# One-core decoder layer: the first two batches normalised in halves with their copies and first projections in another order, and the last product's last two batches in PSUM tiles of their own

## The chip, the cores and the metric

The kernel runs on one core of a Trainium2 chip; the other seven cores are idle. The metric is the device time of one execution in microseconds (us). The core has five engines, each with a queue of instructions that it works off in order: TensorE (PE, matrix products; the loading of weights is listed as PEld), VectorE (DVE), ScalarE (ACT), GpSimd (POOL), and SyncE (SP), which here only issues transfers (DMAs). They wait for one another through semaphores. PE writes its results to PSUM; DVE and ACT carry them from there to SBUF.

## The reference

A decoder layer in float32 over x of shape 16 x 128 x 1024 (16 batches of 128 tokens, 1024 features):

```python
x = x + attn(layernorm(x))          # one head of width 256, softmax over 128 keys
x = x + xattn(layernorm(x), ctx, ctx)   # 8 heads, linear attention over the channels
x = x + ffn(layernorm(x))           # int4 weights, dequantised; silu(gate) * up, then down

# the parts that the change touches
def layernorm(x, eps=1e-5):
    return (x - mean(x)) / sqrt(var(x) + eps)
def attn(x):                        # qkv: 1024 -> 3 * 256
    q, k, v = split(x @ Wqkv + bqkv)
    return softmax(q @ k.T / sqrt(256)) @ v @ Wo + bo
def ffn(x):                         # inter = 2752
    return (silu(x @ Wg.T) * (x @ Wu.T)) @ Wd.T
```

## The kernel before

**The stages.** Self-attention comes first; cross-attention and the dequantising of the weights follow; the feed-forward network takes most of the time. Its products are built by a fast scheme with seven smaller products in place of eight, at two levels, so a part of a result is a sum of several products that stay in PSUM or in SBUF tiles until the last one is there.

**The start (lines 361 to 431 and 523 to 543).** SP's queue loads the first four batches of x, then the weights `wqkv` in five pieces, `bv`, the next four batches, `wo`, the bias `bo_sb` (128 copies of one row, line 379), and the last eight batches. Self-attention works in four groups of four batches (512 tokens), the loop `for t in range(NT)`. For a group, each batch is normalised to `xn` (128 tokens x 1024), turned by eight 128 x 128 transposes on PE into two PSUM tiles `tr` (four transposes each), and copied into the group's `xnT`: the first half by DVE, the second half by ACT. The pool of `tr` tiles has three, and the pool of `xn` has two, so the sixth `tr` needs the copy of the third to be over, and so on.

The first group has a function of its own, `first_rows` (line 396). DVE takes the statistics of a half batch at a time (`half`: BATCH_NORM_STATS2), then the aggregate, and DVE and POOL form the reciprocal deviation `rstd` (POOL raises to the power -0.5, line 153); ACT normalises the batch in one instruction of 1024 columns (`rows`), PE turns it, ACT copies the second half and DVE, one batch later, the first half (`copy`). The wrapper `InOrder` keeps the DVE instructions in the order in which they are written; instructions without it are ordered by the framework's scheduler.

Then the projection of queries and keys: four output parts f, each over eight chunks of features. For the first group each part is made in two halves, first the 256 tokens of batches 0 and 1, then those of batches 2 and 3 (`query_key` with `tokens`). One chunk of 256 tokens is two matmul instructions in the trace, so half a part is 16. Between the second halves of the parts stand, for f = 0 to 3: `add_bias(f)` on POOL (line 434: X[b] = X[b] + bo_sb, 128 x 1024, in place) and `turn` of batch 4 + f, whose normalising is done by DVE (line 156, `xn<-X,mv,rstd`). Before the projection stand the statistics of batches 4 to 7 and one `row_rstd` for all four (lines 152 and 153, a row of 128 x 4).

**The end (lines 1922 to 1998).** The down projection ends with the seven inner products `INNER = (1, 5, 6, 7, 3, 4, 2)` of the last outer product. A PSUM tile `po` holds four batches x 256 columns. Product 2 is accumulated on the tile of product 1. In the last product the first two batches are multiplied, and `got` adds them to the sum `u` and sends them out; then the other two in the same tile, the same way. Batches 0 and 2 leave through ACT's queue, 1 and 3 through SP's.

Of the kernel before, what the change touches and what calls it, by code (L numbers as in the profile page):

```python
# [12 lines left out]
F32 = mybir.dt.float32  # L13
# [6 lines left out]
P = 128  # L20
# [63 lines left out]
def decoder_layer(  # L84
# [59 lines left out]
    def row_stats(b, vector=nc.vector):  # L144
        st = small.tile([P, 2, 6], F32, name="bnst")
        for h in range(2):
            vector.bn_stats(st[:, h, :], X[b][:, ts(h, 512)])
        vector.bn_aggr(mv[:, b, :], st)

    def row_rstd(b0, n, vector=nc.vector, gpsimd=nc.gpsimd):  # L150
        r = rstd[:, ds(b0, n)]
        vector.tensor_scalar(r, mv[:, ds(b0, n), 1], EPS, None, ALU.add)
        gpsimd.tensor_tensor(r, r, mhalf[:, :n], ALU.pow)
# [14 lines left out]
    def normalise_act(dst, src, b, scalar=nc.scalar):  # L168
        scalar.activation(
            dst, src, AF.Identity, bias=shift[:, b : b + 1], scale=rstd[:, b : b + 1]  # L170
        )
# [183 lines left out]
    with (  # L355
# [27 lines left out]
        def turn_half(xn, xnT, b, h):  # L383
            tr = atr.tile([P, 4, P], F32, name="tr")
            for j in range(4):
                nc.tensor.transpose(tr[:, j, :], xn[:, ts(4 * h + j, P)], ident)  # L386
            return xnT[:, ts(h, 4), ts(b % BPT, S)], tr
# [8 lines left out]
        def first_rows(xnT):  # L396

            vector = InOrder(tc, nc.vector)
            halves = {}

            parts = {}

            def half(b, h):
                if h == 0:
                    parts[b] = small.tile([P, 2, 6], F32, name="bnst")
                vector.bn_stats(parts[b][:, h, :], X[b][:, ts(h, 512)])
                if h == 1:
                    vector.bn_aggr(mv[:, b, :], parts[b])
                    row_rstd(b, 1, vector)

            def rows(b):
                xn = a2.tile([P, C], F32, name="xn")
                row_shift(b, vector)
                normalise_act(xn, X[b], b)
                halves[b] = turn_half(xn, xnT, b, 0)
                nc.scalar.copy(*turn_half(xn, xnT, b, 1))

            def copy(b):
                vector.tensor_copy(*halves[b])

            half(0, 0)
            half(0, 1)
            for b in range(1, BPT):
                half(b, 0)
                rows(b - 1)
                if b > 1:
                    copy(b - 2)
                half(b, 1)
            rows(BPT - 1)
            copy(BPT - 2)  # L430
            copy(BPT - 1)

        def add_bias(b):
            nc.gpsimd.tensor_tensor(X[b], X[b], bo_sb, ALU.add)
# [86 lines left out]


        xnTs = [a2.tile([P, CC, TB], F32, name="xnT")]
        first_rows(xnTs[0])
        oT = None
        for t in range(NT):
            xnT = xnTs.pop()
            more = t + 1 < NT
            if more:
                xnTs.append(a2.tile([P, CC, TB], F32, name="xnT"))  # L530
                for b in range((t + 1) * BPT, (t + 2) * BPT):
                    row_stats(b)
                row_rstd((t + 1) * BPT, BPT)
            qkT = a2.tile([P, 4, TB], F32, name="qkT")
            halves = {}
            if t == 0:

                for f in range(4):
                    halves[f] = aps.tile([P, TB], F32, name="mm")
                    query_key(f, xnT, qkT, halves[f], ts(0, TB // 2))  # L540
            for f in range(4):
                if t == 0:
                    query_key(f, xnT, qkT, halves[f], ts(1, TB // 2))
                else:
                    query_key(f, xnT, qkT)
                add_bias(t * BPT + f)
                if more:
                    if oT is not None:
                        give((t - 1) * BPT + f, oT)
                    turn((t + 1) * BPT + f, xnTs[0])  # L550
                if t > 0:
                    for _ in range(2 if t == 2 else 1 + f % 2):
                        next(early, None)
            v = a2.tile([P, BPT, DH], F32, name="v")
            value(0, xnT, v)
            at = weigh(qkT)
            if more:
                value(1, xnT, v)
                value(2, xnT, v)
                atT = turn_weights(at)  # L560
                value(3, xnT, v)
                if t == 0:
                    for _ in range(3):
                        next(early)
            else:
# [1222 lines left out]
    with ExitStack() as dst:  # L1788
# [125 lines left out]
        for n, oq in enumerate(DOWN):  # L1914
            (lr, wr), (_, _, L, W) = rem, now
            direct(*now)
            after = None
            if n + 1 < len(DOWN):
                rem = remainder(DOWN[n + 1])
                keep_sums()  # L1920
                load_left(DOWN[n + 1], rem)
                after = operands(DOWN[n + 1])
                load_left(DOWN[n + 1], rem, True)
            bank, kept = {}, {}

            def multiply(bank, pairs, start, stop, rows=range(BPT)):
                for i in rows:
                    for c, (l, w) in enumerate(pairs):
                        nc.tensor.matmul(  # L1929
                            bank[:, i, :],  # L1930
                            l[:, ts(i, S)],
                            w,

                            start=(start and c == 0 and i % 2 == 0),
                            stop=(stop and c == len(pairs) - 1),
                            skip_group_check=True,
                        )

            for iq in INNER:
                set_ = {2: 1, 3: 5, 4: 7}.get(iq, iq)  # L1940
                if set_ == iq:
                    bank[iq] = dps[iq].tile(wide, F32, name=f"po{iq}")
                pairs = [(L[iq, i], W[iq, i]) for i in range(NI)]

                more = {2: (0, 0), 3: (0, 1), 4: (1, 0)}.get(iq)
                if more is not None:
                    pairs.append((lr[more[0]], wr[:, ts(more[1], OW)]))
                ps = bank[set_]
                if oq == DOWN[-1] and iq == INNER[-1]:
                    put_outs()  # L1950
                    for rows in (range(2), range(2, BPT)):
                        multiply(ps, pairs, False, True, rows)
                        got(oq, (0, 0), ps, only=rows)
                    break
                multiply(ps, pairs, set_ == iq, iq == 6 or more is not None)
                put_outs()
                if iq == 1:
                    t = kept["u"] = dt.tile(wide, F32, name="iu")
                    nc.scalar.copy(t, ps)
                elif iq == 5:  # L1960
                    combine(3, *now)
                    for ib in ((1, 1), (0, 1), (1, 0), (0, 0)) if oq == 4 else ():
                        vector.tensor_tensor(U[ib], U[ib], residual(oq, ib), ALU.add)
                elif iq == 6:
                    t = kept["u"]
                    vector.tensor_tensor(t, ps, t, ALU.add)
                    kept["v"] = dt.tile(wide, F32, name="iv", bufs=1)
                    vector.tensor_tensor(kept["v"], bank[5], t, ALU.add)
                elif iq == 7:
                    extra = dps[6].tile(wide, F32, name="po6")  # L1970
                    multiply(extra, [(lr[1], wr[:, OW:])], True, True)
                    got(oq, (1, 1), ps, kept["v"], extra)
                elif iq == 3:
                    got(oq, (0, 1), ps, kept["u"])
                elif iq == 4:
                    got(oq, (1, 0), ps, kept["u"])
                else:
                    got(oq, (0, 0), ps)
                if after is not None and iq in (3, 4, 2):
                    combine({3: 5, 4: 6, 2: 7}[iq], *after)  # L1980
            now = after
# [74 lines left out]
```

## Time and profile before

Three runs took 2171.88 us in the median (2171.53 to 2173.71). The profiled execution took 2173.11 us, with a span of 2171.3 us from its first to its last record.

| engine | busy us | share of the span |
|---|---|---|
| PE matmul | 2153.8 | 99% |
| PE weight loads | 1643.8 | 76% |
| DVE | 1556.3 | 72% |
| POOL | 803.9 | 37% |
| ACT | 525.5 | 24% |

| stretch, us | PE busy us of | DVE busy us | POOL busy us | DMA engines busy |
|---|---|---|---|---|
| 0 to 8.2 | 0.00 of 8.20 | 3.73 | 1.48 | 78% |
| 8.2 to 18.1 | 9.38 of 9.90 | 5.51 | 1.44 | 96% |
| 18.1 to 33.5 | 15.40 of 15.40 | 12.15 | 6.22 | all |
| 33.5 to 47.5 | 14.00 of 14.00 | 11.23 | 14.00 | 42% |
| 47.5 to 63.6 | 16.10 of 16.10 | 7.89 | 6.42 | 1% |
| 2159 to 2166 | 5.45 of 7.00 | 1.03 | 0.00 | 13% |

A row of the timeline is: start and duration in us, engine, line of the code, operation, what it writes from what it reads, shape, count, and in brackets how long the engine had been idle and what ended that. When a row has a count over 1, the duration is that of the whole group. A row of the chain has its start, its length, and the engine, tile and line. Matmuls overlap their neighbours, so the ends of PE rows are modelled.

### The profile page before, as it was taken

To read this page: it belongs to the slowest core of one execution; us is meant where nothing else is said; L and a number is where in the kernel's file an instruction comes from. 1 tells how busy PE (TensorE), PEld (TensorE's weight loads), DVE (VectorE), ACT (ScalarE), POOL (GpSimd) and SP (SyncE) were. 2 spreads that over 40 slices of the span, in tenths; PEclk is the share of its full clock that TensorE was granted. 3 is DMA by queue.
4 is the path that set the end of the run, shared out by engine and by line. 5 is a ranking of instruction groups with operands and counts; after the bars stand their busy time and mean duration, and the time that the engine had idled before them with its cause. 6 is when DMAs were issued, how large, how long until landed. Compare 5 with 4: busy or idle time off the path is not lost.

```text
span 2171.3 us, 25688 instructions
## 1 busy us (share of the span) xinstructions
PE 2153.8 (99%) x9004; PEld 1643.8 (76%) x9004; DVE 1556.3 (72%) x2098; ACT 525.5 (24%) x710; POOL 803.9 (37%) x675
## 2 busy tenths in 40 slices
PE   8999999999999999999999999999999999999998
PEld 7565655555555568888888888888886888888887
DVE  7899578888888758786777987878774445534573
ACT  2111235655665541211221212112111000000000
POOL 5454124333433345544444545444441022323200
PEclk9999999999999999999999999999999999999999
DMA  6446447777797676878888746677667578979941
GB/s 259 150 131 219 154 136 237 236 226 236 223 276 242 191 237 217 288 254 262 264 282 290 228 150 209 209 238 237 201 206 237 182 206 242 282 197 254 265 128 60
DMA packets 272203, 474.56 MB, mean 219 GB/s; under 512 B 29633, under 2 KB 128321, under 8 KB 266177
## 3 DMA queue, kind: packets, MB, share of 16 engines
q1 hardware_dynamic: 226736, 383.02, 54.6%
q0 software_dynamic: 27456, 71.45, 12.1%
q10 hardware_dynamic: 17872, 18.36, 2.6%
q8 instruction: 74, 1.21, 0.2%
q14 instruction: 65, 0.52, 0.1%
HBM read 314.64 MB, written 157.55 MB: 217 GB/s over the span
## 4 chain that ended last, share of the span: by engine, by line
PE 95%; DVE 3%; issue 1%; ACT 0%; POOL 0%; DMA 0%; DVEq 0%; POOLq 0%; ACTq 0%
PE q L80 38%; PE po L1929 22%; PE kq L80 10%; PE mm L80 8%; PE kx L80 5%; PE mm L441 4%; PE p L80 3%; PE mm L456 2%; PE mm L335 1%; DVE pa L80 1%; PE tr L386 0%; DVE C L80 0%; DVE pc L80 0%; PE mm L471 0%; PE mm L511 0%
## 5 line engine op out<-in xcount | busy, mean ns | idle before, releaser
L80 PE MATMUL q<-ti,li 128*128 128x256 f32 x1680 | 385.4, 379 | 0.0
L80 PEld LDWEIGHTS q<-ti,li 128*128 128x128 f32 x1680 | 319.2, 190 | 43.4
L80 ACT COPY k<-q 128x512 f32<-128x512 f32 x210 | 122.9, 585 | 660.7 <-PE q L80 645.7
L80 POOL TENSOR_TENSOR li<-w 128x512 f32<-128x512 f32 x140 | 203.8, 1461 | 52.2 <-PE q L80 31.6
L872 POOL TENSOR_TENSOR qe<-qe,qrec 128x1024 f32<-128x1024 f32 x64 | 146.2, 2284 | 175.2 <-DVE qrec L80 156.6
L80 POOL TENSOR_TENSOR li<-w,li 128x512 f32<-128x512 f32 x70 | 107.9, 1541 | 259.5 <-PE q L80 235.5
L1929 PE MATMUL po<-wc,lc 128*128 128x256 f32 x840 | 183.4, 379 | 0.0
L1929 PEld LDWEIGHTS po<-wc,lc 128*128 128x128 f32 x840 | 159.6, 190 | 21.8
L80 DVE TENSOR_TENSOR C<-q,k 128x512 f32<-128x512 f32 x150 | 102.7, 685 | 70.2 <-PE q L80 65.8
L80 PE MATMUL q<-b,w 128*128 128x256 f32 x640 | 151.2, 379 | 0.0
L80 POOL TENSOR_TENSOR li<-li,w 128x512 f32<-128x512 f32 x70 | 91.6, 1309 | 122.2 <-PE q L80 121.8
L80 PEld LDWEIGHTS q<-b,w 128*128 128x128 f32 x640 | 121.6, 190 | 17.0 <-issue 0.5
L80 PE MATMUL q<-ti,w 128*128 128x256 f32 x560 | 132.3, 379 | 0.0
L1929 PE MATMUL po<-wq,lq 128*128 128x256 f32 x560 | 126.8, 379 | 0.8 <-DVE m L80 0.8
L80 PEld LDWEIGHTS mm<-qs,m_sb 128*128 128x128 f32 x512 | 97.3, 190 | 40.1 <-issue 29.7
L80 PE MATMUL kx<-ek,cxt 128*128 128x512 f32 x256 | 121.8, 598 | 0.0
L80 DVE STREAM_TRANSPOSE kt<-qe 128x1024 f32<-128x1024 f32 x64 | 79.2, 1238 | 58.8 <-POOL qe L872 54.6
L80 PE MATMUL mm<-qs,m_sb 128*128 128x256 f32 x512 | 120.8, 379 | 0.0
L80 PE MATMUL kq<-wq_sb,xn 128*128 128x512 f32 x256 | 120.2, 593 | 0.4 <-ACT qe L860 0.4
L80 PE MATMUL kq<-wk_sb,cx 128*128 128x512 f32 x256 | 120.1, 592 | 0.0
L1929 PEld LDWEIGHTS po<-wq,lq 128*128 128x128 f32 x560 | 106.0, 190 | 16.7 <-DVE m L80 1.2
L80 DVE TENSOR_TENSOR pa<-pa,sz 128x1024 f32<-128x1024 int32 x86 | 116.4, 1354 | 2.1
(203 smaller groups left out, 3712.2 us busy)
## 6 DMA issues: line engine op xcount, KB each, us to landing
ti<-r SPq DMA_DIRECT2D x36, 1024.0 KB, 7.4
w<-wg SPq DMA_DIRECT2D x140, 256.0 KB, 3.3
w<-wu SPq DMA_DIRECT2D x140, 256.0 KB, 3.8
lq<-h SPq DMA_DIRECT2D x140, 256.0 KB, 5.3
kd<-kt SPq DMA_DIRECT2D x62, 512.0 KB, 3.7
qs<-kd SPq DMA_DIRECT2D x244, 128.0 KB, 3.2
h<-h SPq DMA_DIRECT2D x80, 256.0 KB, 3.1
wq<-wd SPq DMA_DIRECT2D x70, 256.0 KB, 7.4
```

The source lines that it names most:

```text
L80: return lambda *args, **kw: self._tc.keep_in_program_order(fn(*args, **kw))
L335: tensor.matmul(ps, oT[:, d, ts(b % BPT, S)], wo_d[d][:, ts(h, 512)], start=(d == 0), stop=(d == 1),)
L441: nc.tensor.matmul(ps[:, tokens], wqkv_sb[:, f, c, :], xnT[:, c, tokens], start=(c == 0), stop=(c == CC - 1),)
L456: nc.tensor.matmul(ps, xnT[:, c, ts(i, S)], wqkv_sb[:, 4:6, c, :], start=(c == 0), stop=(c == CC - 1),)
L872: nc.gpsimd.tensor_tensor(qe, qe, rec.unsqueeze(2).to_broadcast(wide), ALU.mult)
L1929: nc.tensor.matmul(bank[:, i, :], l[:, ts(i, S)], w,  start=(start and c == 0 and i % 2 == 0), stop=(stop and c == len(pairs) - 1), skip_g ...
```

## The change

It has two parts.

At the start, batches 0 and 1 are normalised in two instructions of 512 columns each, into tiles of their own. The transposes and copies of a batch are a step of their own, `turn_rows`. The function becomes a generator: it stops after the normalising of batch 3 is written, and the caller resumes it after the first and after the second part of the first projections, so that the transposes of batches 2 and 3 stand behind parts 0 and 1. DVE's copy of batch 1 is placed ahead of the statistics of batch 3. The statistics of batches 4 to 7 are written behind the first projections, and in the first group they are kept in order on DVE.

At the end, the sum `u` takes up batches 2 and 3 of product 1 early, by an added DVE instruction after product 5, and product 2 of these two batches goes to two PSUM tiles of its own (those of `po6` and `po5`, free by then), one batch at a time.

```diff
+            normed = {}
+
             def rows(b):
-                xn = a2.tile([P, C], F32, name="xn")
                 row_shift(b, vector)
-                normalise_act(xn, X[b], b)
-                halves[b] = turn_half(xn, xnT, b, 0)
-                nc.scalar.copy(*turn_half(xn, xnT, b, 1))
+                xn = normed[b] = [
+                    a2.tile([P, C], F32, name="xn") for _ in range(2 if b < 2 else 1)
+                ]
+                n = C // len(xn)
+                for h, t in enumerate(xn):
+                    normalise_act(t[:, ts(h, n)], X[b][:, ts(h, n)], b)
+
+            def turn_rows(b):
+                halves[b] = turn_half(normed[b][0], xnT, b, 0)
+                nc.scalar.copy(*turn_half(normed[b][-1], xnT, b, 1))
...
             half(0, 0)
             half(0, 1)
-            for b in range(1, BPT):
-                half(b, 0)
-                rows(b - 1)
-                if b > 1:
-                    copy(b - 2)
-                half(b, 1)
-            rows(BPT - 1)
-            copy(BPT - 2)
-            copy(BPT - 1)
+            half(1, 0)
+            rows(0)
+            turn_rows(0)
+            half(1, 1)
+            half(2, 0)
+            rows(1)
+            turn_rows(1)
+            copy(0)
+            half(2, 1)
+            copy(1)
+            half(3, 0)
+            rows(2)
+            half(3, 1)
+            rows(3)
+            yield
+            turn_rows(2)
+            copy(2)
+            yield
+            turn_rows(3)
+            copy(3)
...
-        first_rows(xnTs[0])
+        opening = first_rows(xnTs[0])
+        next(opening)
...
+            if t == 0:
+
+                for f in range(4):
+                    halves[f] = aps.tile([P, TB], F32, name="mm")
+                    query_key(f, xnT, qkT, halves[f], ts(0, TB // 2))
+                    next(opening, None)
             if more:
                 xnTs.append(a2.tile([P, CC, TB], F32, name="xnT"))
                 for b in range((t + 1) * BPT, (t + 2) * BPT):
-                    row_stats(b)
+                    row_stats(b, InOrder(tc, nc.vector) if t == 0 else nc.vector)
                 row_rstd((t + 1) * BPT, BPT)
-            qkT = a2.tile([P, 4, TB], F32, name="qkT")
-            halves = {}
-            if t == 0:
-
-                for f in range(4):
-                    halves[f] = aps.tile([P, TB], F32, name="mm")
-                    query_key(f, xnT, qkT, halves[f], ts(0, TB // 2))
...
-                            start=(start and c == 0 and i % 2 == 0),
+                            start=(start and c == 0 and (i % 2 == 0 or len(rows) == 1)),
...
-                    for rows in (range(2), range(2, BPT)):
-                        multiply(ps, pairs, False, True, rows)
-                        got(oq, (0, 0), ps, only=rows)
+                    multiply(ps, pairs, False, True, range(2))
+                    got(oq, (0, 0), ps, only=range(2))
+                    for i, q in ((2, 6), (3, 5)):
+                        own = dps[q].tile(wide, F32, name=f"po{q}")
+                        multiply(own, pairs, True, True, (i,))
+                        got(oq, (0, 0), own, only=(i,))
                     break
...
+                    if oq == DOWN[-1]:
+                        apart = U[0, 0][:, 2:]
+                        vector.tensor_tensor(apart, bank[1][:, 2:], apart, ALU.add)
```

More of the change, by code (lines that the diff above doesn't have):

```diff
@@ L528, in decoder_layer @@
             more = t + 1 < NT
-            if more:
-                xnTs.append(a2.tile([P, CC, TB], F32, name="xnT"))
-                for b in range((t + 1) * BPT, (t + 2) * BPT):
-                    row_stats(b)
-                row_rstd((t + 1) * BPT, BPT)
             qkT = a2.tile([P, 4, TB], F32, name="qkT")
@@ L540, in decoder_layer @@
                     query_key(f, xnT, qkT, halves[f], ts(0, TB // 2))
+                    next(opening, None)
+            if more:
+                xnTs.append(a2.tile([P, CC, TB], F32, name="xnT"))
+                for b in range((t + 1) * BPT, (t + 2) * BPT):
+                    row_stats(b, InOrder(tc, nc.vector) if t == 0 else nc.vector)
+                row_rstd((t + 1) * BPT, BPT)
             for f in range(4):
```

## The prediction

> **What bounds the kernel now.** I read the page's table of engines first, then what PE waits for, then the chain of the first 50 us and of the last 15, and last the timeline of POOL and DVE between 26 and 50 us, because the compiled order of the changed kernel moves an instruction on POOL's queue there.
>
> PE is busy for 2153.8 of 2171.3 us. All of its waits on the page:
>
> ```profile
> PE tr L386 <- ACT xn L169: 8.2, 1, 8.2
> PE po L1929 <- DVE m L80: 0.8, 1, 0.8
> PE q L80 <- DVE C L80: 0.5, 1, 0.5
> PE mm L441 <- DVE xnT L80: 0.5, 1, 0.5
> PE kq L80 <- ACT qe L860: 0.4, 1, 0.4
> PE mm L511 <- DVE v L463: 0.4, 1, 0.4
> ```
>
> The columns are total us, times, longest. So the middle is PE alone; only the two ends can give time back, and a wait put into PE's stream at the start is not made up later: no later wait is long enough. The chain at the start:
>
> ```profile
> 12.55 2.08 PE mm L441 x4
> 14.63 1.71 PE tr L386 x8
> 16.34 1.08 PE mm L441 x4
> 17.41 0.87 PE tr L386 x8
> 18.29 15.54 PE mm L441 x72
> 33.83 0.87 PE tr L386 x8
> 34.70 3.46 PE mm L441 x16
> 38.16 0.87 PE tr L386 x8
> ```
>
> From 18.29 PE never stops; eight transposes cost 0.87 and 16 matmuls 3.46. Before that a matmul costs about 0.43 instead of 0.216: PE's clock is still half, although the column of the granted clock shows 1.00 there. The chain at the end:
>
> ```profile
> 2158.52 0.77 DVE m L80 x2
> 2159.28 0.04 issue
> 2159.33 5.47 PE po L1929 x24
> ```
>
> PE waits 0.85 us for DVE to read batches 0 and 1 out of the tile that it writes next. And POOL with DVE:
>
> ```profile
> 26.48 1.02 POOL L153 TENSOR_TENSOR rstd<-rstd,mhalf 128x4 f32<-128x4 f32 x1 [12.32 <-DVE rstd L152]
> ...
> 28.30 5.12 POOL L434 TENSOR_TENSOR X<-X,bo_sb 128x1024 f32<-128x1024 f32 x2 [0.80 <-DMA bo_sb<-in_bo]
> ...
> 28.26 2.94 DVE L156 TENSOR_SCALAR xn<-X,mv,rstd 128x1024 f32<-128x1024 f32 x1
> ...
> 40.09 0.77 DVE L152 TENSOR_SCALAR rstd<-mv 128x4 f32<-128x4 f32 x1
> ...
> 46.86 2.36 POOL L434 TENSOR_TENSOR X<-X,bo_sb 128x1024 f32<-128x1024 f32 x1
> 46.92 2.85 DVE L156 TENSOR_SCALAR xn<-X,mv,rstd 128x1024 f32<-128x1024 f32 x1 [2.63 <-POOL rstd L153]
> ```
>
> The bias adds cannot start before 28.30, when `bo_sb` lands (the DMA engines are all busy until then). They start every 2.32 us. DVE's `xn` takes 0.81 us beside an idle POOL, but 2.3 to 2.9 once the adds run: it ends about 0.59 us after the add that was running (28.26 + 2.94 = 31.20 against the next add at 30.62). The add after that is pushed back (2.77 instead of 2.32). Even the tiny row L152 takes 0.77 instead of 0.17, until the next add starts at 40.79. DVE and POOL exclude each other here.
>
> **The change part by part: the start.** Normalising in halves: a 512-column ACT instruction lies between the 0.58 of a 512-column copy and the 1.24 of the full one; I take 0.65. The first transposes then start at 7.6 instead of 8.21, batch 1's follow at about 9.5, DVE's copy of it ends near 11.3 instead of 12.5, and the first matmul starts at 11.35 (12.55 if the first piece of `wqkv`, which is there by 12.55, lands no earlier). At 0.43 each until 16.1 and 0.216 after, half a part ends near 17.1; with two batches of transposes (1.74), part 1 (3.46) and 48 matmuls (10.4), PE reaches the transposes of batch 4 at about 32.6 instead of 33.83. Two more ACT instructions, the moved copy and DVE's order lie behind this PE work.
>
> Taken alone, that is 1.2 us of gain. But batch 4 must be normalised by then. The compiled order of POOL in the changed kernel is: the four single powers, *then add_bias(0)*, then the power for batches 4 to 7, then add_bias(1) and so on. Before, the power came first and ran at 26.48, in time. Now it stands behind an add that waits for `bo_sb` until 28.30. Also, the statistics of batches 4 to 7 stand behind the copy of batch 3 on DVE, which needs transposes that now come near 21.5: they start at about 22.6 instead of 20.49, take the same 5.74, and L152 arrives at 28.3, when the add has begun or just before.
>
> So: add 28.30 to 30.62; L152 until 30.7; power 30.77 to 31.76 (0.99 from 45.87 to 46.86); add_bias(1) follows at once, as at 46.86, and DVE's `xn` 0.06 behind it, as at 46.92. It ends at 31.76 + 2.32 + 0.59 = 34.67. PE, free at 32.6, turns batch 4 at 34.72, against 33.83: 0.9 us late instead of 1.2 early.
>
> Late next is DVE. The `xn` of batch 5 waits for the next add: 34.08 + 2.77 + 0.59 = 37.44. Then DVE's compiled order has five statistics and an aggregate (3.3) and the copy of batch 4's first half, which ends at 41.3. PE meanwhile: 34.72 + 0.87 + 3.46 = 39.05; four transposes of batch 5 until 39.49; the other four need the `tr` tile that this copy frees. They start at 41.34; a second wait, 1.85. Part 2 ends at 45.24, half of batch 6 at 45.68, and the other half needs the copy of batch 5's first half. On DVE that stands behind `xn` of batch 6 (ends 41.93 + 0.59 = 42.52), three statistics, three aggregates and L152 of batches 8 to 11, which comes at 44.9. The adds start at 39.61, 41.93 and 44.69 (2.76 again): L152 comes 0.2 late for the gap and waits, as at 40.09, until 47.05. The copy ends at 47.65; third wait, 2.0. Part 3 then ends at 51.59, batch 7 at 52.46. There the values start (47.69 before): 4.75 us late. From here nothing on DVE or POOL is further behind than PE is, so I add nothing.
>
> POOL's later stores of weights come 10 us and more after the adds (67.70), and the queue of SP keeps its order: 0. Bounds of the start: the waits cannot be below what the order of POOL forces with everything else hidden, 0.9 us late at batch 4; and not above 4.75 plus one more turn of the lock (2.8), 7.5. I take 4.75, since each step repeats a row; the 0.2 us of the third wait is its weakest point.
>
> **The end.** The tiles of batches 2 and 3 are free (their last readers ran at 2132 and 2142), so the 0.85 us goes. After the last matmul one add of 0.41 stands instead of two in 0.76: 0.35. Sum 1.2. The added DVE instruction (128 x 512; 0.68 by the rows of that size) sits after product 5, where DVE has 123 of 240 us to do and PE's next need of its results is products away: 0, at worst 0.68. Bounds: 0.5, to 1.5 if the last transfer, now alone, lands a little earlier. I take 1.2.
>
> **A rule weighed.** The timeline shows half speed until PE has worked on products for 3.5 us. The Trainium skill (TensorE: Matmul & The Clock Gate, Part 1) says that an idle window of about 3.4 us brings the half clock back. By the page the three waits, 1.85 to 2.1 us, would cost only themselves and the sum would stay; without it, the one row that shows a wait on a warm PE (0.85 at the end, then ten matmuls in the usual 2.4) speaks the same way for a shorter wait, and rival B has the price if longer ones do bring half speed back.
>
> **Sum.** 4.75 - 1.2 = +3.55 us. On the profiled execution: 2173.11 + 3.55 = 2176.7. That execution lies 1.2 above the median of the runs; on the median it is 2171.88 + 3.55 = 2175.4, which I forecast. It is 0.16% above before. I count within 0.2%, 4.3 us, as what a measurement can't tell from no change, so the likeliest verdict is "same", on its slow side.
>
> **The rivals.**
> *A: the third wait is missed.* L152 gets in before the add; the copy of batch 5 ends at 45.65, the wait falls away: the values start at 50.44, +2.75 - 1.2 = +1.55: 2173.4. For it: only 0.2 us decide. Against it: the whole chain moves with the adds, so an earlier start doesn't help.
> *B: the clock falls in the waits.* At the start half speed lasted some 3.5 us from 12.55, which is eight matmuls at an extra 0.216, 1.73 us, for each wait. One to three of these: +5.3 to +8.7, 2177.2 to 2180.6, slower. For it: the matmuls at 12.55 ran at 0.43 after 4 us of transposes. Against: the matmuls after the 0.85 us at the end are not slower.
> *C: faster, the start works as drawn.* If the power of batches 4 to 7 comes before 32.6 less 0.8, because `bo_sb` lands 2.5 us earlier or because the lock lets DVE through, PE keeps its 1.2: -1.2 - 1.2 = -2.4: 2169.5. It decides at batch 4's `xn` ending by 32.6. Against it: the DMA engines are full until 28 and their order is the same. That the first part doesn't do what it is drawn for, an early PE start, is no rival: that start comes, and is spent.
>
> **How the numbers follow.** The forecast 0.50, A 0.25, B 0.17, C 0.08. The range leaves C out below and most of B's upper part: 2172.4 (A, less 1 us of scatter between runs) to 2178.2 (B with one fall, plus 1). Slower by over 0.2% (above 2176.2): nearly all of B, and a fourth of the forecast by scatter, 0.29; faster (below 2167.5): 0.03, from C with a better end; within: 0.68.
>
> **What would show it.** In the changed profile: a POOL bias add at 28.3 ahead of the 128x4 power, which runs near 30.8; the first `xn` of DVE ending near 34.7; PE waits on DVE before the transposes of batches 4, 5 and 6 of about 2 us each, the last one absent in A; the first matmul near 11.4; matmuls of 0.216 after the waits (0.43 in B); the values starting near 52.5; and at the end no PE wait before the last two batches. It is wrong if the power runs before 28 us, or if DVE's `xn` doesn't wait for the adds.

## The result, and the profile after

The changed kernel takes 2176.42 us in the median of 18 runs (2175.13 to 2178.53), the kernel before, on the same chip, 2173.04 us in 18 runs (2171.22 to 2174.44). The ratio is 1.0019 with a 95% interval of 1.0012 to 1.0025: some 3.4 us slower in the medians, just inside the 0.2% that was set as the limit of "same". The profiled execution took 2176.10 us with a span of 2174.3 us, 3.0 us more than the span of before.

First what PE waits for (total us, times, longest us):

```profile
PE tr L386 <- ACT xn L169: 7.8, 2, 7.5
PE tr L386 <- DVE xnT L393: 3.4, 2, 2.0
PE tr L386 <- DVE xn L156: 1.6, 1, 1.6
PE q L80 <- DVE C L80: 0.5, 1, 0.5
PE kq L80 <- ACT qe L881: 0.4, 1, 0.4
PE mm L530 <- DVE v L482: 0.4, 1, 0.4
```

Two rows are new, the second and the third: 5.0 us in three waits in front of transposes. One row is gone: PE no longer waits for DVE at `po` (0.8 before). Next the timeline of POOL and DVE, in order of time:

```profile
27.18 2.35 POOL L453 TENSOR_TENSOR X<-X,bo_sb 128x1024 f32<-128x1024 f32 x1 [13.26 <-DMA bo_sb<-in_bo]
27.66 1.90 DVE L152 TENSOR_SCALAR rstd<-mv 128x4 f32<-128x4 f32 x1
29.63 1.03 POOL L153 TENSOR_TENSOR rstd<-rstd,mhalf 128x4 f32<-128x4 f32 x1
30.63 15.26 POOL L453 TENSOR_TENSOR X<-X,bo_sb 128x1024 f32<-128x1024 f32 x6
30.70 5.59 DVE L156 TENSOR_SCALAR xn<-X,mv,rstd 128x1024 f32<-128x1024 f32 x2 [1.14 <-POOL rstd L153]
...
43.58 2.34 DVE L152 TENSOR_SCALAR rstd<-mv 128x4 f32<-128x4 f32 x1
45.83 0.68 DVE L393 COPY xnT<-tr 128x512 f32<-128x512 f32 x1
```

One bias add now stands on POOL ahead of the power of batches 4 to 7. It starts the moment `bo_sb` lands (27.18). DVE's 128 x 4 instruction, 0.17 us by itself, comes 0.48 us into the add and lasts 1.90, until the add is over. The power can run only then. Its place behind the add is enough for that: in a second profile of this kernel (below) the small instruction came at 26.94, ahead of the add, took its 0.17, and the power still ran only at 30.42, behind the add of 28.10. So the power is late, and the first two `xn` of DVE take 5.59 us for two, each drawn out by an add. At 43.58 the same small instruction is caught again, now for 2.34 us, and the copy behind it starts at 45.83. PE shows what each of these costs:

```profile
33.66 1.06 PE L386 MATMUL tr<-ident,xn 128*128 128x128 f32 x8 [1.59 <-DVE xn L156]
...
39.98 0.66 PE L386 MATMUL tr<-ident,xn 128*128 128x128 f32 x4 [1.36 <-DVE xnT L393]
...
46.56 0.66 PE L386 MATMUL tr<-ident,xn 128*128 128x128 f32 x4 [2.04 <-DVE xnT L393]
47.05 3.62 PE L460 MATMUL mm<-xnT,wqkv_sb 128*128 128x256 f32 x16
...
51.38 3.62 PE L475 MATMUL mm<-wqkv_sb,xnT 128*128 128x256 f32 x16
```

Waits of 1.59, 1.36 and 2.04 us, 4.99 in all. A wait is counted from the modelled end of the row before it, which lies 0.16 us behind the start of an undisturbed next row, so the waits delay PE by somewhat more than their sum. The 16 matmuls after the last of them take 3.62, the duration of an undisturbed group: the clock did not fall. The values start in the chain at 51.55 (47.69 before): 3.86 us late. (The chain counts a matmul from the end of the row before it; in the timeline the same starts are 51.38 and 47.53. Starts of the values are from the timeline from here on, unless the chain is named.) And the end, from the chain:

```profile
2099.98 67.54 PE po L1950 x312
2167.52 0.02 issue
2167.54 0.42 DVE m L80
```

PE runs through to its last matmul, and one add of 0.42 us follows instead of two. Matched instruction by instruction, PE is 3.84 us behind before until the last product and 2.72 us behind at its end: the end gives PE 1.12 us.

### The profile page after: what moved, and what is told of

Its sections match the earlier page's. It is cut to its first block, busy times and chain, and to the rows that moved or that the text cites. A ratio compares the mean times of both kernels' runs of the same rounds, so it can differ in the third digit from the quotient of the medians.

```text
span 2174.3 us, 25693 instructions
## 1 busy us (share of the span) xinstructions
PE 2153.3 (99%) x9004; PEld 1643.0 (76%) x9004; DVE 1557.9 (72%) x2099; ACT 525.9 (24%) x712; POOL 803.3 (37%) x675
## 4 chain that ended last, share of the span: by engine, by line
PE 93%; DVE 3%; DMA 1%; issue 1%; ACT 0%; POOL 0%; ACTq 0%; SPq 0%; POOLq 0%; DVEq 0%
PE q L80 38%; PE po L1950 22%; PE kq L80 10%; PE mm L80 8%; PE kx L80 5%; PE p L80 3%; PE mm L460 3%; PE mm L475 2%; PE mm L335 1%; DVE pa L80 1%; DMA bv_sb<-in_bv 1%; DMA X<-in_x 1%; DVE bnst L147 0%; DVE C L80 0%; DVE xn L156 0%
```

## The experiments

The theories: (T) the whole loss comes from one bias add that the scheduler puts ahead of the power of batches 4 to 7 on POOL, and from DVE waiting on POOL behind it; (A) the third wait is a race and can fall away; (B) the waits let the clock fall; and, as the rival to T, that the loss lies in the new order of the copies and projections itself. Each ratio is to the kernel before on the same chip, with its 95% interval.

**The end alone.** The kernel before, with only the hunks of the last product.

```diff
 before.py, and of the change only
+                    for i, q in ((2, 6), (3, 5)):
+                        own = dps[q].tile(wide, F32, name=f"po{q}")
...
+                    if oq == DOWN[-1]:
+                        apart = U[0, 0][:, 2:]
+                        vector.tensor_tensor(apart, bank[1][:, 2:], apart, ALU.add)
```

> The kernel before with only the end of the change. Theory: the PE wait of 0.85 us before the last two batches goes and one add instead of two stands behind the last matmul, so DVE's last add ends 1.2 us earlier against the start of the last product; what the last transfer gives back is open (0 to 0.6 us): -0.6 to -1.2 us against before. Rival: the span's end is set by something behind the last transfer, and nothing is gained.

2171.43 us against 2171.74; 0.9998 (0.9989 to 1.0007). The wait of 0.85 us is gone: PE, 0.5 us behind the first profile of before until the last product, is 0.6 us ahead of it at its end. The second thing that was removed, one of DVE's two last adds (0.34 us), is given back in part: after the last add the span runs on for 5.63 to 6.34 us in ten profiles with the new end (mean 5.95), for 5.66 to 5.87 in four with the old (mean 5.77). The medians show 0.3 us, less than the 0.6 to 1.2 that were expected, and nothing that can be told from no gain; PE's time in the profile shows 1.1 us. The single runs say more than the median: five of the eleven took 2169.85 to 2170.72, and the fastest of the 28 runs of before took 2171.35.

**The start alone.** The changed kernel, with the end as before.

```diff
 after.py, without the hunks of the last product
-                            start=(start and c == 0 and (i % 2 == 0 or len(rows) == 1)),
+                            start=(start and c == 0 and i % 2 == 0),
...
+                    for rows in (range(2), range(2, BPT)):
+                        multiply(ps, pairs, False, True, rows)
+                        got(oq, (0, 0), ps, only=rows)
```

> The changed kernel without the change of the end. Theory: the loss of the start alone, +3.9 us at the values (51.55 against 47.69), and no gain at the end: +3.9 us against before (ratio 1.0018), 0.6 to 1.2 slower than the changed kernel. Rival: the end costs something elsewhere, and the start alone is +3.4 or less.

2178.46 us; 1.0030 (1.0019 to 1.0040), more than was expected. In the profile PE is 5.4 us behind, not 3.9. The timeline of PE at the third wait:

```profile
46.40 0.85 PE L386 MATMUL tr<-ident,xn 128*128 128x128 f32 x4 [2.04 <-DVE xnT L393]
47.04 5.15 PE L460 MATMUL mm<-xnT,wqkv_sb 128*128 128x256 f32 x16
```

The same wait of 2.04 us, but the 16 matmuls after it take 5.15 us, 1.53 more than the 3.62 of the changed kernel, and that is the size of the difference between 5.4 and 3.9. The table of stretches, for 47 to 52 us (the busy time and number of PE, weight loads, DVE, ACT and POOL, then the granted clock):

```profile
47.00:52.00 5.00, 5.00 (x18) 4.12 (x17) 2.93 (x3) 0.58 (x1) 4.33 (x3) 0.69 0.00 2
```

The clock stands at 0.69 there, against 1.00 in the same stretch of the changed kernel. This is rival B, with one fall, in this execution.

**The power first.** The changed kernel, with the power of batches 4 to 7 kept ahead of the bias adds on POOL. Nothing else is touched in the source. In the trace PE's order is the same, and POOL's but for this power; on DVE one statistic and one aggregate of batches 8 to 11 also come earlier than in the changed kernel.

```diff
-            nc.gpsimd.tensor_tensor(X[b], X[b], bo_sb, ALU.add)
+            (InOrder(tc, nc.gpsimd) if b < 4 else nc.gpsimd).tensor_tensor(X[b], X[b], bo_sb, ALU.add)
...
-                row_rstd((t + 1) * BPT, BPT)
+                row_rstd((t + 1) * BPT, BPT, gpsimd=InOrder(tc, nc.gpsimd) if t < 1 else nc.gpsimd)
```

> The changed kernel, with the power for batches 4 to 7 put back ahead of the bias adds on POOL. Theory: power at 27.9, the first xn of DVE ends near 31.8, before PE needs it at 32.1, so the first wait (1.6 us) goes; the adds still run beside DVE's xn, so a wait of about 1.5 us before the second half of batch 5's transposes and one of about 2.0 before those of batch 6 remain; the values start near 49.5 instead of 51.55: -2.0 us against the changed kernel, +1 to +1.5 against before. Rival (POOL's order is all of it, the lock is not): all three waits go and the values start near 45.9: -5.6 against the changed kernel, -2.2 against before.

2172.0 us; 0.9997 (0.9988 to 1.0006). This edit takes some 4 us off the changed kernel's time (2176.42 to 2172.0 in the medians), and the loss is gone; +1 to +1.5 us against before had been expected. Of the waits one is left:

```profile
PE tr L386 <- ACT xn L169: 7.5, 1, 7.5
PE tr L386 <- DVE xnT L393: 1.7, 1, 1.7
```

The first wait went, as drawn. That the third went too was not expected: POOL and DVE read

```profile
27.46 1.02 POOL L80 TENSOR_TENSOR rstd<-rstd,mhalf 128x4 f32<-128x4 f32 x1 [13.66 <-DVE rstd L152]
28.45 10.21 POOL L80 TENSOR_TENSOR X<-X,bo_sb 128x1024 f32<-128x1024 f32 x4
...
41.34 0.17 DVE L152 TENSOR_SCALAR rstd<-mv 128x4 f32<-128x4 f32 x1
```

The small DVE instruction met a gap between two adds at 41.34 and took its 0.17. That is rival A's mechanism. It seems to go with the order on DVE: in all three profiles that have the changed kernel's order on both engines (the changed kernel twice and the start alone) the small instruction comes 0.03 us after an add has started, lasts 2.34 and leaves a wait of 2.04, while in the next two experiments, which have the add in front but two DVE instructions moved as here, it takes 0.70. The median is not all of it: three of the eleven runs took 2168.79 to 2169.59, the other eight 2171.55 to 2172.99, and the profile is of one of the eight (2172.0). What went differently in the three is not on record.

**The add first, without the change.** The reverse: the kernel before, with one bias add ahead of that power and nothing of the change.

```diff
 before.py
+                if t == 0:
+                    add_bias(0)
-                row_rstd((t + 1) * BPT, BPT)
+                row_rstd((t + 1) * BPT, BPT, gpsimd=InOrder(tc, nc.gpsimd) if t == 0 else nc.gpsimd)
...
-                add_bias(t * BPT + f)
+                if t + f > 0:
+                    add_bias(t * BPT + f)
```

> The kernel before, with one thing of the change alone: add_bias(0) is put ahead of the power for batches 4 to 7 on POOL's queue. Theory (POOL's order makes the waits): add at about 27.2 to 28.3, power behind it, the first xn of DVE ends at 33.4 to 34.7 instead of 28.35, PE waits before the transposes of batches 4 to 6 and the values start at 51.5 to 52.5 instead of 47.69: +3.9 to +4.75 us against before (ratio 1.0018 to 1.0022). Rival (the new order of PE and the later statistics make them): the power still finds its input early, the transposes of batch 4 come within 0.5 us of 33.83, and the time is that of before within 1 us.

2176.6 us against 2171.74; 1.0020 (1.0011 to 1.0030). By the medians +4.9 us. In time, the order that the change brings about as a side effect costs by itself as much as the whole change. (Here too one statistic and one aggregate on DVE change places besides.) Its profile has

```profile
26.78 2.35 POOL L80 TENSOR_TENSOR X<-X,bo_sb 128x1024 f32<-128x1024 f32 x1 [12.90 <-DMA bo_sb<-in_bo]
...
30.16 5.61 DVE L156 TENSOR_SCALAR xn<-X,mv,rstd 128x1024 f32<-128x1024 f32 x2 [5.27 <-POOL rstd L80]
```

the same two `xn` for 5.6 us as in the changed kernel. PE had one wait of 2.02 us at the transposes there, where three had been expected, and the values start at 49.28, not at 51.5 to 52.5. Its span of 2174.4 is 3.1 above that of before, and 1.2 of that comes much later, with a wait of 0.80 us at 1183 us that the profiles of before don't have.

One distance leaves out whatever happened ahead of the waits: from the start of PE's last matmul ahead of batch 4's transposes to the start of the values. It is 14.08 and 14.07 us in the two profiles of before, which have no wait there.

| kernel | last matmul starts, us | values start, us | distance, us | above 14.08 |
|---|---|---|---|---|
| before, first and second profile | 33.45, 31.72 | 47.53, 45.79 | 14.08, 14.07 | 0 |
| changed, first and second profile | 31.70, 30.98 | 51.38, 52.17 | 19.68, 21.19 | 5.6, 7.1 |
| the power first | 31.25 | 47.32 | 16.07 | 2.0 |
| the add first, without the change | 32.90 | 49.28 | 16.38 | 2.3 |
| whole rows (next) | 31.74 | 49.07 | 17.33 | 3.3 |
| the adds later (below) | 31.43 | 45.51 | 14.08 | 0 |

So the add ahead of the power costs 2.3 us at the start of the old kernel, and the power put first takes 3.6 to 5.1 of the 5.6 to 7.1 off the changed one. This settles T against its rival as far as the new order of copies, halves and projections goes: by itself it does not cost the time. It is not quite the one order on POOL alone, though. The third wait, 2.04 of the 5.6, stands in full only in the profiles that have both the add ahead of the power and the changed kernel's order on DVE; no run has that DVE order with the power first.

**Whole rows.** The changed kernel, with batches 0 and 1 normalised in one instruction each.

```diff
-                    a2.tile([P, C], F32, name="xn") for _ in range(2 if b < 2 else 1)
+                    a2.tile([P, C], F32, name="xn") for _ in range(1)
```

> The changed kernel with batches 0 and 1 normalised in one instruction each again. Theory (the early start is spent in the wait for batch 4): the first transposes start about 0.6 us later, PE reaches batch 4's transposes at 32.5 to 32.9 instead of 32.1, its wait there shrinks by as much, and from the end of that wait all is the same: the time of the changed kernel within 0.3 us, +3.4 against before. Rival (the early start counts): +0.6 us against the changed kernel.

2174.54 us; 1.0011 (1.0002 to 1.0020). The expectation of "as the changed kernel within 0.3" missed by about 2 us. The halves do not cost them: without them the scheduler also writes DVE's later instructions in another order, and in the timeline

```profile
42.90 0.70 DVE L152 TENSOR_SCALAR rstd<-mv 128x4 f32<-128x4 f32 x1
```

the small instruction waits for 0.5 us only. PE's waits are 1.51 in front of batch 4 and one more of 1.32, instead of 1.36 and 2.04: the mechanism of rival A, though what is left is one wait in front of batch 6 rather than the one in front of batch 5. DVE's order moved only behind 39 us, so the rows before that do say what the halves are worth: with whole rows the first transposes start at 7.95 instead of 7.49, but PE's first product at 11.79 (11.85 and 11.77 with halves), and its last matmul ahead of batch 4 at 31.74 (31.70 in the first profile with halves, where PE came up to full speed at the same time, 14.0). The halves brought PE nothing by then. What the whole changed start is worth is asked below.

**The adds later.** The changed kernel, with the adds of batches 0 to 3 placed behind the power of batches 8 to 11, so that no add lies beside the first eight `xn`.

```diff
-                add_bias(t * BPT + f)
+                if t > 0:
+                    add_bias(t * BPT + f)
...
+            if t == 0:
+                for b in range(2 * BPT, 3 * BPT):
+                    row_stats(b)
+                row_rstd(2 * BPT, BPT, gpsimd=InOrder(tc, nc.gpsimd))
+                for b in range(BPT):
+                    add_bias(b)
...
 (the adds of batches 0 to 7 and the powers are kept in order on POOL)
```

> The changed kernel, with both powers (batches 4 to 7 and 8 to 11) ahead of all bias adds on POOL; the adds of batches 0 to 3 start only behind the second, and those of 4 to 7 move into the next group. Theory: no bias add runs while DVE normalises batches 4 to 6, each xn takes about 0.8 us, the three waits go, PE reaches the transposes of batch 4 at 32.1 and the values at about 45.9 instead of 47.69 before: with the end's gain -2.2 to -2.7 us against before (ratio 0.9988 to 0.9990). Rival (the start gives nothing even without the waits): the values start at 47.7 or later and only the end's -0.6 to -1.2 is left. A third way: the adds of batches 4 to 7 now run beside DVE's work on the weights after 60 us and PE waits there.

2178.97 us; 1.0033 (1.0021 to 1.0045). The start is what was expected: two `xn` in 1.53 us, the values at 45.51. But PE now waits elsewhere:

```profile
28.70 1.53 DVE L156 TENSOR_SCALAR xn<-X,mv,rstd 128x1024 f32<-128x1024 f32 x2 [1.13 <-POOL rstd L80]
...
125.74 1.09 PE L520 MATMUL tr<-ident,at 128*128 128x128 f32 x4 [5.27 <-DVE at L512]
126.62 5.08 PE L475 MATMUL mm<-wqkv_sb,xnT 128*128 128x256 f32 x16
```

5.27 us for DVE's normalising of the attention weights of the second group, 2.18 for those of the third, and the matmuls behind the first of them are slow (granted clock 0.64 between 126 and 131 us). The values start 2.0 us ahead of the first profile of before (0.3 ahead of the second), and the new waits spend more than that. The expectation had named such waits as a third way, without a price.

**All eight adds there.** The same, with the adds of batches 4 to 7 in that place as well.

```diff
-                for b in range(BPT):
+                for b in range(2 * BPT):
                     add_bias(b)
...
-                if t > 0:
+                if t > 1:
                     add_bias(t * BPT + f)
```

> As with the adds put later, but all the adds of batches 0 to 7 stand directly behind the second power on POOL, and none of them moves into the next group. Theory: the start is the same as there, DVE's xn of batches 4 to 7 run free of the adds and PE has no wait before the transposes, the values start near 45.6, 2.0 us ahead of before; the adds end near 62 as DVE's work on the weights begins, so that the PE waits of 5.3 and 2 us near 125 and 192 us go; with the end's 1.1: about -3.1 us against before (ratio 0.9986). Rival (the power of the third group, now in order behind these adds, or the adds beside DVE after 55 us, keep PE waiting): a PE wait of over 1 us between 60 and 200 us, and the time of before or above it.

2171.94 us; 0.9998 (0.9989 to 1.0007), where 0.9986 had been expected: the sign of the rival, a wait of over 1 us before 200 us and the time of before. The values start at 45.13, the long wait at 126 us is gone, and the shorter one remains:

```profile
PE tr L386 <- ACT xn L169: 7.7, 2, 7.6
PE tr L520 <- DVE at L512: 2.2, 1, 2.2
```

**The third group's power free again.** The same, except that the power of batches 12 to 15 is no longer kept in order on POOL, which leaves DVE's order around the attention of later groups as in the changed kernel.

```diff
-                    row_rstd((t + 1) * BPT, BPT, gpsimd=InOrder(tc, nc.gpsimd))
+                    row_rstd((t + 1) * BPT, BPT, gpsimd=InOrder(tc, nc.gpsimd) if t == 0 else nc.gpsimd)
```

> The kernel of e7 (additions 0 to 7 behind the powers of the second and third group on GpSimd's queue), but the third group's power is free in its place again, so that VectorE's order of the attention's normalisations is that of the changed kernel. My theory, that the 2.16 us wait of TensorE near 185 us in e7 came from that order: the start is as in e7 (values near 45.1 to 45.6 us against 47.69 in the first profile of before, no wait of TensorE in front of the transposes of batches 4 and 5), no wait near 185 us on the attention's normalisation, TensorE done some 2.2 us + 1.1 us = 3.3 us ahead of the first profile of before, time 0.9985 to 0.9992 of before (about 2169 to 2170 us). Rival: the wait belongs to the later additions themselves, it stays at about 2.2 us, and the time is before's within 0.0005.

2170.49 us against 2171.94; 0.9992 (0.9983 to 1.0001). The wait near 185 us is gone:

```profile
PE tr L386 <- ACT xn L169: 7.5, 1, 7.5
PE mm L530 <- DVE v L482: 1.1, 1, 1.1
PE q L80 <- DVE C L80: 0.5, 1, 0.5
```

All eleven runs (2169.51 to 2170.80) lie below the fastest of the fifteen of before beside them (2171.30). PE ends 2.3 us ahead of the first profile of before, not the 3.3 expected: at 126 us it waits 1.14 for the values `v` (0.39 in the changed kernel), 0.75 us more. The wait went, so its cause is not the later adds by themselves. The cause that was offered, DVE's order, has a weak side in the timelines: in this kernel DVE ends its instruction at L512 at 184.12 and PE wants it at 184.27, with 0.15 us to spare, while in the kernel of the run before it ended at 184.74 and PE had come 1.5 us sooner. A later PE takes part in its going away; how much of the 2.2 us is due to the order is left open.

**Once more, and with the old start.** The last kernel again, and beside it the kernel before with those later adds and the new end, that is the last kernel without the changed start.

```diff
 the second kernel: before.py, the end of the change, and
-                add_bias(t * BPT + f)
+                if t > 1:
+                    add_bias(t * BPT + f)
...
 (the statistics, powers and adds as in the last kernel)
```

> The kernel of e9 once more, beside the next one: 2170 to 2171 us, 0.9985 to 0.9998 of before, values at 45.1 to 45.7 us and no wait of TensorE in front of the transposes of batches 4 to 7, whichever clock its first matmuls get.

> The kernel before with the later additions of e9 and the change at the end of the last product, but with the first batches as before (whole rows, projections behind all four batches): what is left out against e9 is the changed start alone. Before's own start had no wait in front of batches 4 and 5, so the later additions have nothing to give here. Theory: the values start at 45.8 to 47.7 us as in the two profiles of before, the end gives 1.1 us less what its last stores give back, 2171 to 2172.5 us, 0.0002 to 0.001 above e9: the changed start is worth nothing to 2 us, by the clock of the first matmuls. Rival: the changed start is worth its whole 2.2 us in every execution, and this kernel is 0.001 above e9 or more.

2171.41 us, 0.9991 (0.9982 to 1.0000), and 2170.91 us, 0.9992 (0.9983 to 1.0001). The values start at 44.79, a little earlier than the expected range, and at 46.38. In these two profiles the changed start is 1.6 us earlier, but not by itself: PE's matmuls come up to full speed at 11.4 us in the first and at 14.5 in the second. In time the two kernels can't be told apart, so the rival, 2.2 us in every execution, finds no support. These versions are the fastest that were run, about 0.0008 under the kernel before; one interval touches 1 and the others cross it, and here, unlike in the run before, the single times overlap with those of before (fastest 2171.64), so it is likely, but not settled, that they beat it.

**Both kernels again.** The changed kernel and the kernel before, unaltered, for the scatter of the profiles.

> The changed kernel unaltered, on the chip of this group. Theory: the same three waits; the values near 51.5 when L152 misses the gap between two adds and about 2 us earlier when it doesn't, 1.5 us later when PE's clock falls behind a wait; +3.4 us against before in the middle. Rival (the difference was one of the chip): the ratio moves by more than 0.1% from 1.0019.

> The kernel before unaltered, on the chip of this group, as the base for the landmarks of the other two. Theory: the values start within 0.5 us of 47.69, PE has one wait of 0.85 us at the end, ratio 1.0000 with an interval of 0.1%. Rival: the values start a microsecond earlier here, and differences against the first profile are too small by that.

2176.85 us, 1.0022 (1.0013 to 1.0032), and 2171.66 us, 0.9999 (0.9990 to 1.0008). The spans were 2174.6 and 2169.9. The second profile of the changed kernel has

```profile
28.10 2.36 POOL L453 TENSOR_TENSOR X<-X,bo_sb 128x1024 f32<-128x1024 f32 x1 [14.37 <-DMA bo_sb<-in_bo]
30.42 1.02 POOL L153 TENSOR_TENSOR rstd<-rstd,mhalf 128x4 f32<-128x4 f32 x1
...
26.94 0.17 DVE L152 TENSOR_SCALAR rstd<-mv 128x4 f32<-128x4 f32 x1
```

In it `bo_sb` lands at 28.10 instead of 27.18, the first wait is 3.09 us instead of 1.59 and the values start at 52.17 instead of 51.38; in the second profile of before the values start at 45.79 instead of 47.53, earlier than the theory allowed. The ratio of the changed kernel moved by 0.0003 only, so the chip is not the difference. But by the medians of this group the change costs 5.0 us, and 1.0022 lies just outside the 0.2%: whether the loss is more or less than 0.2% is not settled. More on both below.

## Why the prediction was right

The forecast was 2175.4 us, +3.55, "same" on its slow side; the medians give +3.4, and +5.0 in the repeat. The main steps hold; two terms vary between executions by a microsecond and more (the landing of `bo_sb`, and the clock of PE's first matmuls), and the base was not a typical one.

| step | predicted, us | measured, us |
|---|---|---|
| first matmul | 11.35 | 11.85 |
| PE reaches batch 4's transposes | 32.6 | 32.07 |
| first bias add starts | 28.30 | 27.18 |
| power of batches 4 to 7 starts | 30.77 | 29.63 |
| transposes of batch 4 start | 34.72 | 33.66 |
| waits one, two, three | 2.1, 1.85, 2.0 | 1.59, 1.36, 2.04 |
| values start (chain) | 52.46 | 51.55 |
| end: PE, and one add of DVE less | 0.85 + 0.35 | 1.12 + 0.34, less 0.18 in the last stores |

**The early start comes and is spent, but it is smaller than drawn.** PE reached batch 4 some 1.8 us before the 33.83 of the kernel before, and then waited. Most of the 1.8 is not the change: PE's matmuls came up to full speed at 14.0 us there and at 16.8 in that profile of before. In the two second profiles both came up at 12.6, and the last matmul ahead of batch 4 starts at 30.98 against 31.72: 0.7 us, where the prediction has 1.2. Its halves of 512 columns took 0.81, not 0.65, and the run with whole rows shows nothing that they brought PE.

**The order on POOL is the main cause.** It was read from the compiled order, not from the diff, and the two experiments that move it (the power first in the changed kernel, the add first in the old one) turn the loss in time off and on. It is the best supported step of the prediction. From reaching batch 4 to the values the prediction has 52.46 - 32.6 = 19.9 us; the chain gives 51.55 - 32.07 = 19.5 in the first profile and 52.34 - 31.36 = 21.0 in the second.

**Late next is DVE.** Both further waits stand on the copies it was foreseen they would stand on. The third was lost by a hair: the add started at 43.55, the small instruction came at 43.58. The hair was the same 0.03 us in all three profiles with this order, though the adds themselves began up to 1.1 us apart: what the prediction held against rival A, that the whole chain moves with the adds, is what held. The step was still the weakest: in three other kernels (whole rows, the add first, the power first), where two of DVE's instructions stand elsewhere, the small instruction took 0.17 to 0.70.

**The term that was off** is the landing of `bo_sb`. The prediction took one value, 28.30, from the one profile of before. It landed at 27.18 in the first profile of the changed kernel, at 28.10 in its second, and at 26.78, 26.99 and 27.13 in three other kernels whose first add waits for it. The chain behind it moves with it: against the first profile of before the start costs 3.86 us in the first profile and 4.65 in the second, where the prediction had 4.75. The sum should have carried this landing as a range of over 1 us, not as a row.

**The end** gave PE 1.12 us where its wait alone was put at 0.85 (0.16 of the rest is the modelled end of the row ahead of the wait), and gave back on the mean half of the 0.34 of DVE's add: about 1.1 + 0.34 - 0.18 = 1.3 us on the mean, against 1.2. In the first profile, whose last stores were the longest, 3.0 us of loss are left in the span.

That the forecast still lies at the measured difference is luck in part. The profiled execution of before belongs to the longer ones: a second profile starts the values 1.7 us earlier. The four pairs of spans (2174.3 and 2174.6 against 2171.3 and 2169.9) give +3.0 to +4.7; the medians give +3.4 and +5.0.

**Rival B** was priced at 1.73 us for each fall and rejected on a wait of 0.85 us. It did not happen in either profile of the changed kernel, and did happen in the kernel with the start alone, with a price of 1.53. It was not excluded by the rows that there were. The price rested on a reading that fails: the prediction has half speed until PE has worked on products for 3.5 us, but the second profile of before is at full speed 0.3 us after its first product (12.28, 12.60). How often the fall comes in the changed kernel is open: four of its ten repeated runs (2177.99 to 2178.69) lie 1 us and more above the other six (2176.10 to 2176.97), and none of the four was profiled. The Trainium skill (TensorE: Matmul & The Clock Gate, Part 1) has half clock after an idle window of about 3.4 us. Here a wait of 5.27 us did bring it, and one of 3.09 did not, which agree; one of 2.04 brought it in one execution of three that had it at the same place, which does not. Nor does counting from product to product, transposes included, sort them: 3.28 us (43.76 to 47.04) where the clock fell, about 4.0 (31.36 to 35.35) where it did not fall.

**Rival C** needed the power ahead of the add. The power-first run puts it there, and at 0.9997 does not reach the -2.4 of that rival, because in its profile the second wait (1.70) stays. Three of its eleven runs, 2.15 to 2.95 us under the median of before, do come to about that; no profile says why.

## What to carry to other kernels

An engine whose work is not on the path can still hold one small instruction that is: look in the compiled order of every queue that the change moves work past, not only in the diff, for a long instruction that gets ahead of a short one that others wait for. Where two engines exclude each other, a short instruction costs what is left of the long one it meets, so its cost is a matter of a few hundredths of a microsecond in when it comes, and a forecast should carry both cases; here two instructions moved on the same queue decided it, not the execution. When a wait is removed near the start, follow the new order to the next groups (here to 126 and 185 us) before counting the gain.

## What the runs showed of the hardware

**The clock of the first matmuls differs between executions of the same kernel.** In the first profile of before, four matmuls at 12.55 took 2.08 us; in the second, from the PE timeline,

```profile
12.28 1.13 PE L441 MATMUL mm<-xnT,wqkv_sb 128*128 128x256 f32 x4 [0.35 <-DVE xnT L80]
...
45.79 3.62 PE L456 MATMUL mm<-wqkv_sb,xnT 128*128 128x256 f32 x16
```

they took 1.13. Matmuls follow one another every 0.43 us at first and every 0.216 from 16.8 us on in the one and from 12.6 on in the other, and the column of the granted clock shows 1.00 throughout. Where before starts its values 1.7 us earlier, its whole run is 1.5 us shorter, and on two of the chips the times of the unaltered kernel do gather in two groups, most of them at 2171.3 to 2171.9 and 2172.5 to 2173.5. In the changed kernel the same difference (16 matmuls from 11.8 in 4.03 against 4.66) only makes the first wait longer: PE came 0.7 us sooner and waited 1.5 us more, the other 0.8 being the later landing of `bo_sb`. A kernel that waits for another engine does not profit from a better clock ahead of the wait.

**A 128 x 4 instruction of DVE took 0.17 us by itself and 0.67 to 2.34 us** when it came while POOL worked on a bias add (2.35 by itself, 2.81 beside DVE's work), by how much of the add was left.

**A wait of 2 us can be enough to lose the clock, and 3 us not to:** the same 16 matmuls took 5.15 us after a wait of 2.04 and 3.62 after the same wait in another execution; and 3.62 after one of 3.09. What decides it no run here shows.
